# One load for the attention bias of two heads, from a planned order with new durations and new ranks

## The chip, the core and the metric

The kernel runs on one core of a Trainium2 chip. The core has a matmul engine (TensorE, PE in the profile; PEld is its weight load), VectorE (DVE), ScalarE (ACT), GpSimd (POOL) and SyncE (SP), which here issues nearly all transfers to the core's 16 DMA engines. The metric is the time of one execution on the device in microseconds (us); lower is better.

## What is computed

A transformer layer with a conditioned normalization, followed by an adapter, a rotation and a second adapter, for 8 sequences of 512 tokens and 256 features, with 16 heads of 16 features. Cut to what matters:

```
def _L0_cond_ref(src, src_mask, timestep, attention_bias, ...):
    emb = silu(_sin_emb(timestep)) @ W_ada + b_ada
    x = _ln(src) * (1.0 + scale) + shift
    q, k, v = heads of (x @ Wq + bq), (x @ Wk + bk), (x @ Wv + bv)
    scores = jnp.einsum('bhqd,bhkd->bhqk', q / math.sqrt(HEAD_DIM), k)
    scores = scores + attention_bias
    scores = jnp.where(src_mask, -jnp.inf, scores.astype(jnp.float32))
    probs = jax.nn.softmax(scores, axis=-1).astype(v.dtype)
    ctx = jnp.einsum('bhqk,bhkd->bhqd', probs, v)
    x = x + (ctx @ Wo + bo)
    h = _ln(x) * g2 + beta2
    ff = _gelu2(h @ W1 + b1) @ W2 + b2
    return x + ff

x = _L0_cond_ref(x, mask, ...)
x = adapter(x, domain, L1 weights)    # down, gelu, expert of the domain, up, residual, layernorm
x = rotate pairs of features of x by theta and phi
x = adapter(x, domain, L3 weights)
```

`attention_bias` has 8 x 16 x 512 x 512 elements of four bytes, 134 MB; every element is read once. Everything is float32.

## The kernel before

The attention is cut into 128 units: a sequence `b`, a group `g` of four heads and a tile `qt` of 128 queries. A unit's four heads each have a tile of 128 queries x 512 keys. In `attention` (from line 915), a unit goes through these steps, one instruction (or group of them) per head:

- SP loads the head's bias tile into a buffer of the set `BIAS` (line 924, 256 KB a load). `BIAS` (line 298) has 15 buffers of 128 x 512; `dif` are the unit's four.
- POOL adds the mask's large negative numbers, in place (line 928).
- PE makes the scores of the four heads into four PSUM banks (line 936), side by side in strips of 32 rows.
- DVE subtracts scores and bias into the bias buffer and finds the row's extreme, `low` (line 948); ACT takes the exponential there (line 952).
- The probabilities must be turned. For two heads of a unit (none in most of the first sequence) DVE transposes blocks of 32 (line 963, into `tb`) and four DMAs of 128 KB carry them on (line 972, `pT<-tb`). For the others PE transposes (line 987) and ACT or DVE copies the result to `pT` (line 709, the function `evict`). The last of these reads frees the head's bias buffer.
- After every second unit PE multiplies `pT` with the values (line 1013), and DVE and POOL divide by the sums (lines 1026 to 1042).

Between the units lie the projections of the next sequence (`prepare`, from line 785) and, for each half sequence, the rest of the layer (`finish`: lines 1067, 1076, 1083 and 1092 are the feed-forward block, 775 and lines from 1109 the adapters, 717 and 719 the statistics of a normalization, 731 to 739 its application).

The order is written by a planner in the program itself. Each piece of work is a `Task` with a cost for each engine that could do it, a rank, and, for a DMA, the time that its data takes (`data`). `Plan.run` plays the engines through: whenever an engine is free it takes the ready task of the lowest rank whose buffers can be had, and the task's instructions are emitted in the order so found. On the chip every engine then runs its own instructions in exactly that order, and semaphores make it wait for what it needs. So a duration in this list never is a time on the chip: it only decides what is put ahead of what. `AFTER` is how long after a task's end another engine may see its result. `FLIGHT` is how many DMAs may be under way. `Slots.take` gives out the buffer that has been free for longest; a task that needs buffers takes all of them at its start. `Plan.stir`, called at the end, adds to the rank of each task between two bounds a random number of a given seed and width: a list of (seed, low, high, width).

Of the kernel before, what the change touches and what calls it, by code (L numbers as in the profile page):

```python
# [12 lines left out]
F32 = mybir.dt.float32  # L13
# [7 lines left out]
P = 128  # L21
# [59 lines left out]
class Plan:  # L81
# [3 lines left out]
    AFTER = {PE: 0.22, DVE: 0.14, ACT: 0.16, POOL: 0.12, DMA: 3.95}  # L85
# [70 lines left out]
    def run(self, free_at):  # L156
# [14 lines left out]
        while events:  # L171
# [15 lines left out]
            for e in [e for e in free_at if e in idle]:  # L187
# [26 lines left out]
                for b in new:  # L214
                    b.home, b.slot = b.slots.take()
                t.engine, cost = e, t.costs[e]
# [32 lines left out]
def conditioned_sequence_kernel(  # L249
# [22 lines left out]
    nc = tc.nc  # L272
# [25 lines left out]
    BIAS = slots("bias", 15, [P, S])  # L298
# [407 lines left out]
    def evict(pair, r, w, act=0.47, dve=0.6):  # L706

        plan({ACT: act, DVE: dve}, 0, lambda e: (
            nc.scalar.copy(*pair()) if e == ACT else nc.vector.tensor_copy(*pair())), r, w)  # L709

    def statistics(src, src_keys, ts, at=None):
# [3 lines left out]
        for i, (t, key) in enumerate(zip(ts, src_keys)):  # L715
            st = Buffer(ST)
            plan(DVE, 0.33, lambda t=t, st=st: nc.vector.bn_stats(st.t, src.t[:, t, :]),  # L717
                 [key], [st], at=at[i] if at else 0.0)
            plan(DVE, 0.21, lambda t=t, st=st: nc.vector.bn_aggr(mv.t[:, t, :], st.t),
                 [st], [(mv, t)])  # L720
# [64 lines left out]
    def prepare(b):  # L785
# [4 lines left out]
        else:  # L790
            plan(DMA, 0.42, lambda: nc.sync.dma_start(
                res.t, x[b].rearrange("(t p) d -> p t d", p=P)), [], rk, data=1.7)
            plan(DMA, 0.42, lambda: nc.sync.dma_start(
# [120 lines left out]
    def attention(u, n):  # L914
# [6 lines left out]

        dif = [Buffer(BIAS) for _ in range(4)]
        for j in range(4):
            plan(DMA, 0.54, lambda j=j: nc.sync.dma_start(
                dif[j].t, bias[b, 4 * g + j, qt * P : (qt + 1) * P, :]), [], [dif[j]], data=0.84)
# [16 lines left out]
        plan(PE, 0.98, scores, [(qz, par, c) if n else (qz, par, c, "first"), (kT, c)], sc,  # L942
# [8 lines left out]
        for j in range(4):  # L951
            plan(ACT, 0.61, lambda j=j: nc.scalar.activation(  # L952
# [23 lines left out]
        if turned:  # L976
            plan(DMA, 2.75, moved, [(tb, j) for j in range(turned)], [(pT, i)],
# [41 lines left out]
        plan(PE, 1.77, values,  # L1019
# [15 lines left out]
        plan(DVE, 0.21, lambda: nc.vector.reciprocal(of()[:, :, HD], of()[:, :, HD]),  # L1035
# [11 lines left out]
    def feed_forward(res, rk, ts, store=None):  # L1047
# [50 lines left out]
        plan(DVE, 0.1 + 0.3 * n, lambda: nc.vector.tensor_tensor(  # L1098
# [4 lines left out]
    def adapter(b, l, res, rk, ts):  # L1103
# [32 lines left out]
        plan(ACT, 0.27 * n, hidden, [ps, "hid1", "db"], [hid], mode="gelu")  # L1136
# [153 lines left out]
    for n, u in enumerate(units):  # L1290
# [19 lines left out]
        (388521, 59.4, 64.4, 0.5),  # L1310
        (526635, 99.5, 104.5, 0.3),
        (955239, 98.0, 118.0, 0.5),
        (76748, 107.2, 117.2, 0.5),
        (291160, 124.7, 129.7, 1.0),
        (963473, 114.0, 124.0, 0.3),
        (664487, 54.4, 59.4, 0.3),
        (203363, 125.2, 135.2, 0.3),
        (75368, 112.3, 117.3, 0.5),
        (653452, 55.6, 60.6, 0.15),
        (593813, 126.0, 131.0, 1.0),  # L1320
        (573843, 21.5, 41.5, 0.3),
        (961937, 121.3, 131.3, 0.5),
        (875800, 20.4, 25.4, 0.15),
        (637145, 2.0, 12.0, 0.3),
        (952600, 127.6, 137.6, 1.0),
        (260962, 22.0, 27.0, 0.15),
        (38009, 26.2, 36.2, 0.15),
        (272002, 74.3, 84.3, 0.3),
        (911904, 116.2, 156.2, 0.15),
        (541163, 124.1, 129.1, 0.5),  # L1330
        (844975, 78.6, 88.6, 0.3),
        (346962, 121.8, 126.8, 0.5),
        (101166, 97.2, 107.2, 0.15),
        (373769, 121.5, 131.5, 0.3),
        (978427, 78.1, 88.1, 0.5),
        (387854, 121.1, 141.1, 1.0),
        (228221, 124.5, 134.5, 0.5),
        (633691, 29.4, 34.4, 0.3),
        (193779, 129.6, 134.6, 1.0),
        (179418, 94.4, 99.4, 0.15),  # L1340
        (68732, 33.0, 38.0, 1.0),
        (696729, 123.1, 128.1, 0.5),
# [98 lines left out]
```

## Time and profile before

| | us |
|---|---|
| median of 3 runs | 875.85 (873.74 to 878.02) |
| the profiled execution | 876.24 |
| its span, first to last instruction | 874.4 |

The mean clock granted to PE is 0.994 of full speed. The DMA engines move 221.56 MB, at 253 GB/s in the mean. Groups of instructions that the change bears on, with busy time, mean duration of one, idle time of the engine just before them and what ended most of it:

```profile
L928 POOL TENSOR_TENSOR bias<-bias,neg 128x512 f32<-128x512 f32 x512 | 580.3, 1163 | 13.0 <-DMA bias<-in_bias 10.8
L952 ACT ACTIVATE bias<-bias,low 128x512 f32<-128x512 f32 x512 | 344.5, 720 | 37.5 <-DVE low L948 36.6
L948 DVE CUSTOM_DVE_ANT_0 bias<-bank,bias 128x512 f32<-128x512 f32 x512 | 328.7, 680 | 37.3 <-PE bank L936 28.1
...
L963 DVE STREAM_TRANSPOSE tb<-bias 128x512 f32<-128x512 f32 x232 | 155.8, 692 | 3.6 <-ACT bias L952 3.0
L709 ACT COPY pT<-bank 128x512 f32<-128x512 f32 x229 | 126.7, 584 | 29.5 <-PE bank L987 27.2
```

The left part names line, engine and operation, then output and inputs by the program's names (buffer numbers left out) and their shapes. Every engine but PE idles for more than 95 us in all; the waits shown here are idle time of engines that are not the busiest, and cost nothing by themselves.

```profile
PE 77%; ACT 10%; POOL 5%; DVE 4%; DMA 2%; issue 2%; SPq 0%; POOLq 0%; DVEq 0%; ACTq 0%
```

That is the chain of work that ended last, by engine: followed back from the last instruction, at each step to whatever released it or to the instruction before it on its engine.

### The profile page before, as it was taken

The numbers are of one execution on the slowest core, as the hardware profiler recorded it, in microseconds if no ns is written. First come the engines' busy times: TensorE is split into PE (matmuls) and PEld (weight loads), VectorE is DVE, ScalarE is ACT, GpSimd is POOL, SyncE is SP. The second block draws the span as 40 slices with busy tenths as digits, with TensorE's granted clock in tenths as the row PEclk, the third lists the DMA queues.
The fourth block names the chain that finished last, engine by engine and source line by source line (L and its number), as shares of the span: only waits on it lengthen the run. The fifth ranks groups of instructions, "written<-read, shape, count | busy, mean of one in ns | idle before, by whom it ended". The sixth has DMA issues, their size and how long they took to land.

```text
span 874.4 us, 20307 instructions
## 1 busy us (share of the span) xinstructions
PE 855.0 (98%) x6430; PEld 564.5 (65%) x6430; DVE 778.9 (89%) x2132; ACT 744.4 (85%) x1358; POOL 774.9 (89%) x907
## 2 busy tenths in 40 slices
PE   9999999999999999999999999999999999999994
PEld 7656666566766666667666676666666566666783
DVE  3788888989998999999999889999998999999766
ACT  5987879989898998989989897988889798799653
POOL 8699999999899897999889998998999999899432
PEclk9999999999999999999999999999999999999997
DMA  9698886898988899886986978978996979998300
GB/s 294 192 302 280 280 291 208 232 292 263 311 246 269 252 283 298 260 288 227 294 278 226 292 242 252 317 241 282 283 303 191 291 259 283 303 319 259 103 25 24
DMA packets 163936, 221.56 MB, mean 253 GB/s; under 512 B 18819, under 2 KB 93613, under 8 KB 163782
## 3 DMA queue, kind: packets, MB, share of 16 engines
q1 hardware_dynamic: 163786, 220.25, 79.8%
q8 instruction: 51, 0.84, 0.4%
q14 instruction: 55, 0.45, 0.2%
q10 hardware_dynamic: 44, 0.02, 0.0%
HBM read 152.92 MB, written 7.27 MB: 183 GB/s over the span
## 4 chain that ended last, share of the span: by engine, by line
PE 77%; ACT 10%; POOL 5%; DVE 4%; DMA 2%; issue 2%; SPq 0%; POOLq 0%; DVEq 0%; ACTq 0%
PE bank L936 13%; PE bank L1092 12%; PE bank L987 12%; PE bank L1013 10%; PE bank L1067 9%; PE bank L827 6%; PE bank L775 5%; ACT bias L952 3%; POOL bias L928 3%; PE bank L865 2%; PE bank L751 2%; DMA bias<-in_bias 2%; PE bank L1122 2%; PE bank L421 2%; ACT pT L709 1%
## 5 line engine op out<-in xcount | busy, mean ns | idle before, releaser
L928 POOL TENSOR_TENSOR bias<-bias,neg 128x512 f32<-128x512 f32 x512 | 580.3, 1163 | 13.0 <-DMA bias<-in_bias 10.8
L952 ACT ACTIVATE bias<-bias,low 128x512 f32<-128x512 f32 x512 | 344.5, 720 | 37.5 <-DVE low L948 36.6
L948 DVE CUSTOM_DVE_ANT_0 bias<-bank,bias 128x512 f32<-128x512 f32 x512 | 328.7, 680 | 37.3 <-PE bank L936 28.1
L987 PEld LDWEIGHTS bank<-shifted,bias 128*128 128x128 f32 x1120 | 125.4, 141 | 73.6 <-ACT bias L952 28.8
L987 PE MATMUL bank<-shifted,bias 128*128 128x128 f32 x1120 | 157.5, 277 | 5.1 <-ACT pT L709 2.3
L963 DVE STREAM_TRANSPOSE tb<-bias 128x512 f32<-128x512 f32 x232 | 155.8, 692 | 3.6 <-ACT bias L952 3.0
L709 ACT COPY pT<-bank 128x512 f32<-128x512 f32 x229 | 126.7, 584 | 29.5 <-PE bank L987 27.2
L936 PE MATMUL bank<-kT,qz 32*128 32x512 f32 x1024 | 148.7, 640 | 0.0
L1067 PE MATMUL bank<-hT,w 128*128 128x256 f32 (+1 forms) x544 | 127.9, 375 | 0.5 <-ACT hT L761 0.5
L1013 PE MATMUL bank<-pT,v_pad 128*32 128x256 f32 x1120 | 123.0, 382 | 0.0
L1092 PE MATMUL bank<-w,gT 128*128 128x256 f32 x496 | 118.8, 383 | 0.0
L1067 PEld LDWEIGHTS bank<-hT,w 128*128 128x128 f32 x544 | 94.0, 190 | 29.4 <-issue 8.0
L1013 PE MATMUL bank<-pT,v_turn 128*32 128x256 f32 x928 | 111.4, 382 | 0.3 <-issue 0.3
L1092 PEld LDWEIGHTS bank<-w,gT 128*128 128x128 f32 x496 | 89.9, 190 | 22.6 <-issue 9.6
L1013 PEld LDWEIGHTS bank<-pT,v_turn 128*32 128x32 f32 x928 | 49.1, 109 | 50.9 <-issue 7.8
L936 PEld LDWEIGHTS bank<-kT,qz 32*128 32x128 f32 x1024 | 41.9, 182 | 40.6 <-issue 25.9
L1076 ACT ACTIVATE sig<-bank,b1s 128x256 f32<-128x256 f32 (+1 forms) x136 | 55.4, 455 | 6.4 <-PE bank L1067 4.9
L1083 DVE SCALAR_TENSOR_TENSOR gT<-bank,cols,sig 128x256 f32<-128x256 f32 (+1 forms) x128 | 54.2, 462 | 6.5 <-POOL sig L1079 6.0
L1079 POOL TENSOR_SCALAR sig<-sig 128x512 f32<-128x512 f32 (+1 forms) x68 | 40.3, 594 | 20.1 <-ACT sig L1076 13.3
L1013 PEld LDWEIGHTS bank<-pT,v_pad 128*32 128x32 f32 x1120 | 54.6, 109 | 5.3 <-ACT pT L709 1.7
L717 DVE BATCH_NORM_STATS2 st<-res 128x6 f32<-128x256 f32 x128 | 51.5, 409 | 1.5
L725 POOL TENSOR_TENSOR rstd<-rstd,neg_half 128x2 f32<-128x2 f32 (+2 forms) x59 | 43.4, 735 | 4.9
(138 smaller groups left out, 1101.9 us busy)
## 6 DMA issues: line engine op xcount, KB each, us to landing
bias<-in_bias SPq DMA_DIRECT2D x512, 256.0 KB
pT<-tb SPq DMA_DIRECT2D x464, 128.0 KB
out<-res SPq DMA_DIRECT2D x15, 256.0 KB
res<-in_x SPq DMA_DIRECT2D x7, 512.0 KB
value_rows<-v_pad SPq DMA_DIRECT2D x8, 272.0 KB
v_turn<-value_rows SPq DMA_DIRECT2D x8, 272.0 KB
m<-in_mask SPq DMA_DIRECT2D x8, 256.0 KB
mod<-ada_rows SPq DMA_DIRECT2D x8, 256.0 KB
```

The source lines that it names most:

```text
L709: nc.scalar.copy(*pair()) if e == ACT else nc.vector.tensor_copy(*pair())), r, w)
L928: plan(POOL, 1.12, lambda j=j: nc.gpsimd.tensor_tensor(dif[j].t, dif[j].t, negs[qt].t, ALU.add), [negs[qt]], [dif[j]])
L936: nc.tensor.matmul(sc[j].t, qz.t[strip, par, c, qs], kT.t[strip, c, :], start=True, stop=True,)
L948: plan(DVE, 0.61, lambda j=j: nc.vector.tensor_tensor_reduce(dif[j].t, sc[j].t, dif[j].t, -1.0, 3.0e38, ALU.add, ALU.min, low.t[:, j : j + ...
L952: plan(ACT, 0.61, lambda j=j: nc.scalar.activation(dif[j].t, dif[j].t, AF.Exp, bias=low.t[:, j : j + 1], scale=-1.0), [(low, j)], [dif[j]] ...
L963: plan(DVE, 0.62, lambda j=j: nc.vector.transpose(tb.t.rearrange("p (m h k c) -> h p k m c", m=4, h=TURNED, k=NT)[j], dif[j].t.rearrange(" ...
L987: nc.tensor.transpose(ps.t[:, kc, :], dif[j].t[:, kc * P : (kc + 1) * P], ident)
L1013: nc.tensor.matmul(pv.t[32 * j : 32 * j + 32, :], (v_turn if j < turned else v_pad).t[:, at : at + 32], pj, start=(kc == 0), stop=(kc == N ...
L1067: nc.tensor.matmul(ps.t[:, i, :w], w1[:, c, f * P : (f + 1) * P], hT.t[:, c, :w], start=(c == 0), stop=(c == NC - 1),)
L1076: plan(ACT, 0.155 + 0.1 * n, lambda i=i, f=f, ps=ps, sg=sg: nc.scalar.activation(sg.t[:, i, :w], ps.t[:, i, :w], AF.Tanh, bias=b1s[:, f : ...
L1083: plan(DVE, 0.14 + 0.13 * n, lambda i=i, f=f, ps=ps, sg=sg: nc.vector.scalar_tensor_tensor(gT.t[:, f, :w], ps.t[:, i, :w], cols[:, C_B1 + ...
L1092: nc.tensor.matmul(ps.t[:, i, :], gT.t[:, f, i * P : (i + 1) * P], w2[:, f, :], start=(f == 0), stop=(f == NF - 1),)
```

## The change

The 15 bias buffers become slices of one large tile. From the second unit on, one DMA loads the tiles of two heads: the source is two heads of the same 128 queries, and the destination is the large tile with two slices, whose distance is the stride between them, so that any two free slices can be taken. The planner sorts the slots that a task has taken from one set, so that the first is the lower. The first unit still loads head by head. Besides, durations in the planner's list are changed, and the list for `stir` is replaced: 33 entries with windows of 5 to 40 ranks give way to 21, four of which cover all ranks. The engines' instructions are the same in number and shape; their order, and which buffers they use, is what the planner makes of the new list.

```
-    AFTER = {PE: 0.22, DVE: 0.14, ACT: 0.16, POOL: 0.12, DMA: 3.95}
+    AFTER = {PE: 0.26, DVE: 0.14, ACT: 0.16, POOL: 0.12, DMA: 4.35}
...
                 for b in new:
                     b.home, b.slot = b.slots.take()
+                for home in {b.home for b in new}:
+                    mine = [b for b in new if b.home is home]
+                    for b, slot in zip(mine, sorted(b.slot for b in mine)):
+                        b.slot = slot
...
-    BIAS = slots("bias", 15, [P, S])
+    bias_tiles = const.tile([P, 15, S], F32, tag="bias_tiles", name="bias_tiles")
+    BIAS = Slots([bias_tiles[:, i] for i in range(15)])
...
-    def evict(pair, r, w, act=0.47, dve=0.6):
+    def evict(pair, r, w, act=0.485, dve=0.6):
...
-            plan(DVE, 0.21, lambda t=t, st=st: nc.vector.bn_aggr(mv.t[:, t, :], st.t),
+            plan(DVE, 0.11, lambda t=t, st=st: nc.vector.bn_aggr(mv.t[:, t, :], st.t),
...
+        def two_heads(j):
+            low, high = dif[j].slot, dif[j + 1].slot
+            nc.sync.dma_start(
+                bias_tiles[:, low : high + 1 : high - low],
+                bias[b, 4 * g + j : 4 * g + j + 2, qs].rearrange("h q k -> q h k"))
+
         for j in range(4):
-            plan(DMA, 0.54, lambda j=j: nc.sync.dma_start(
-                dif[j].t, bias[b, 4 * g + j, qt * P : (qt + 1) * P, :]), [], [dif[j]], data=0.84)
+            if n == 0:
+                plan(DMA, 0.54, lambda j=j: nc.sync.dma_start(
+                    dif[j].t, bias[b, 4 * g + j, qs, :]), [], [dif[j]], data=0.84)
+            elif j % 2 == 0:
+                plan(DMA, 0.61, lambda j=j: two_heads(j), [], dif[j : j + 2], data=1.68)
...
-        plan(PE, 0.98, scores, [(qz, par, c) if n else (qz, par, c, "first"), (kT, c)], sc,
+        plan(PE, 1.01, scores, [(qz, par, c) if n else (qz, par, c, "first"), (kT, c)], sc,
...
-            plan(ACT, 0.61, lambda j=j: nc.scalar.activation(
+            plan(ACT, 0.62, lambda j=j: nc.scalar.activation(
...
-            plan(DMA, 2.75, moved, [(tb, j) for j in range(turned)], [(pT, i)],
+            plan(DMA, 2.87, moved, [(tb, j) for j in range(turned)], [(pT, i)],
...
-        plan(PE, 1.77, values,
+        plan(PE, 1.83, values,
...
-    plan.stir([
-        (388521, 59.4, 64.4, 0.5),
...
+    plan.stir([
+        (885440, -99.0, 9999.0, 0.3),
+        (794772, -99.0, 9999.0, 0.3),
+        (765284, -99.0, 9999.0, 0.15),
+        (737822, -99.0, 9999.0, 0.15),
+        (607854, 84.8, 124.8, 0.5),
...
```

The other durations that change: the mask load 0.42 to 0.55, the reciprocal (line 1035) 0.21 to 0.11, the feed-forward block's addition (line 1098) 0.1 + 0.3 n to 0.3 n, and the adapter's gelu (line 1130) 0.27 n to 0.32 n, where n is the number of 128-token tiles.

More of the change, by code (lines that the diff above doesn't have):

```diff
@@ L792, in prepare @@
                 res.t, x[b].rearrange("(t p) d -> p t d", p=P)), [], rk, data=1.7)
-            plan(DMA, 0.42, lambda: nc.sync.dma_start(
+            plan(DMA, 0.55, lambda: nc.sync.dma_start(
                 m8.t, mask[b].rearrange("(t p) k -> p t k", p=P)), [], [m8], data=1.1)
@@ L1034, in attention @@
         of = lambda: sb.t.rearrange("p (b e) -> p b e", e=32)
-        plan(DVE, 0.21, lambda: nc.vector.reciprocal(of()[:, :, HD], of()[:, :, HD]),
+        plan(DVE, 0.11, lambda: nc.vector.reciprocal(of()[:, :, HD], of()[:, :, HD]),
              [], [sb])
@@ L1097, in feed_forward @@
                 plan(PE, 0.86, out_sums, [(gT, f0), (gT, f0 + 1), "w2"], [ps], mode="full")
-        plan(DVE, 0.1 + 0.3 * n, lambda: nc.vector.tensor_tensor(
+        plan(DVE, 0.3 * n, lambda: nc.vector.tensor_tensor(
             res.t[:, here], ps.t[:, :n], res.t[:, here], ALU.add), [ps], rk)
@@ L1135, in adapter @@
         plan(PE, 0.52, down, [*xk, "wd"], [ps], mode="down")
-        plan(ACT, 0.27 * n, hidden, [ps, "hid1", "db"], [hid], mode="gelu")
+        plan(ACT, 0.32 * n, hidden, [ps, "hid1", "db"], [hid], mode="gelu")
         def add(ps):
@@ L1309, in conditioned_sequence_kernel @@
     plan.stir([
-        (388521, 59.4, 64.4, 0.5),
[L1311 to L1342, printed above, removed]
+        (885440, -99.0, 9999.0, 0.3),
[3 more added lines that the diff above has]
+        (607854, 84.8, 124.8, 0.5),
+        (886128, 94.3, 99.3, 0.15),
+        (948330, 89.8, 99.8, 0.3),
+        (583505, 119.4, 159.4, 0.3),
+        (217298, 79.9, 89.9, 0.15),
+        (69777, 126.3, 146.3, 1.0),
+        (254646, 84.9, 94.9, 0.15),
+        (197981, 65.4, 85.4, 0.3),
+        (999944, 72.3, 77.3, 0.5),
+        (86346, 123.5, 128.5, 0.15),
+        (242602, 128.7, 133.7, 1.0),
+        (359993, 55.3, 65.3, 0.15),
+        (117736, 99.0, 109.0, 0.5),
+        (110451, 32.2, 37.2, 0.3),
+        (345240, 19.1, 24.1, 0.15),
+        (895446, 69.8, 74.8, 0.15),
+        (983884, 59.5, 69.5, 0.15),
     ])
```

## The prediction

> **What bounds the kernel.** I read the busy times first, then the busy times by stage, then the waits and the issues of the queue that the change touches, and last the chain of work that ended last.
>
> ```profile
> span 874.4 us, 20307 instructions
> PE 855.0 (98%) x6430; PEld 564.5 (65%) x6430; DVE 778.9 (89%) x2132; ACT 744.4 (85%) x1358; POOL 774.9 (89%) x907
> ```
> PE, the matmul engine, is idle for 874.4 - 855.0 = 19.4 us. The Trainium skill ("Perfetto Trace Analysis", Identifying the Most-Contended Engine) warns that matmul busy time is a poor measure and that the weight load's share, 65% here, is a better one; read so, PE would have about 300 us of room. The trace does not bear that out in the middle of the kernel: there the starts of the 256-column matmuls follow each other at an unchanging 215 ns. So I go by the gaps. The busy times by stage (length, then PE, PEld, DVE, ACT, POOL with their counts, clock, DMA share, GB/s) say where PE idles:
>
> ```profile
> 20.00:130.00 110.00, 107.68 (x853) 69.30 (x846) 88.61 (x250) 90.31 (x167) 99.60 (x103) 1.00 0.83 269
> ...
> 610.00:780.00 170.00, 169.66 (x1310) 109.84 (x1309) 160.21 (x430) 151.17 (x269) 159.63 (x175) 1.00 0.87 275
> ...
> 835.00:875.00 40.00, 28.30 (x178) 21.86 (x176) 25.70 (x74) 18.93 (x53) 12.45 (x33) 0.87 0.06 20
> ```
> From 610 to 780 us PE idles 0.34 us. Over 20 to 835 us the stages give 2.32, 1.01, 0.49, 0.99, 0.49, 0.99, 0.34, 0.16 and 0.00: 6.8 us. The last stage has 11.1 us up to the end of the span; 6.6 of them lie after the last matmul ends (867.8), in the closing normalization and store. "Busy" also hides small losses. Taking each matmul's start to the next start, less the pace of its kind (109 ns for 128 columns, 215 for 256, 429 for 512, about 513 for a row-tiled score pair), I count 275 gaps of about 98 ns where the array's tiling changes (27 us), 382 of about 67 ns where it does not (25.6 us, waits that ended just in time), and 37 of over 115 ns (17.7 us, most of the visible idle included). The last two are what a better order can attack: 43 us in all, spread thin.
>
> **The changed transfer.** Its issues and its waits (duration ns: minimum, median, maximum; then waits of the SyncE queue SPq and of POOL, us in total, times, longest):
>
> ```profile
> L924 SPq DMA_DIRECT2D bias<-in_bias x512: 327/382/2149, 4.5 to 811.3; - x171
> ```
> ```profile
> L972 SPq DMA_DIRECT2D pT<-tb x464: 542/599/1527, 65.4 to 821.5; - x155
> ...
>   PEld bank L1013: 0.8, 3
> ```
> ```profile
> L791 SPq DMA_DIRECT2D res<-in_x x7: 374/425/466, 16.8 to 544.9; - x7
> ```
> ```profile
> POOL bias L928 <- DMA bias<-in_bias: 10.8, 12, 2.6
> ```
> ```profile
> SPq L924 <- PE bank L987: 90.2, 53, 6.6
> ```
>
> Part 1, **fewer issues**. 512 loads of one head become 4 (unit 0) and 254 of two heads. From one start to the next on SPq a load of 256 KB takes 436 ns in the median (382 of it the instruction). A 512 KB load of two heads isn't in the trace. The nearest row is L791, 512 KB from HBM in 1 KB rows: 471 ns from start to start. Bounds: 0.43 us, as the mask load L793 (median 384, start to start 430), and 0.87 us, two of today's. I take 0.47, since L791 moves the same bytes to the same 128 partitions. Saved on SPq: 254 x (0.872 - 0.47) = 102 us, between 0 and 112. It lies beside other work almost whole: the queue is not what PE waits for. Behind a waiting bias load stand the pT<-tb transfers of L972, and those made PE's weight loads at L1013 wait only 0.8 us in 3 times. POOL waited 10.8 us for bias loads. The chain of work shows the places where that mattered:
>
> ```profile
> 524.23 4.31 DMA bias<-in_bias
> ...
> 534.00 4.11 DMA bias<-in_bias
> ```
> ```profile
> 603.06 4.77 DMA bias<-in_bias
> ```
> ```profile
> 788.70 2.67 DMA bias<-in_bias
> ```
> PE idled 0.49, 0.99 and 0.16 us in the stages 520 to 545, 545 to 610 and 780 to 800 that hold these: 1.6 us. So SP's relief is worth 0 to 1.6 us; I take -0.8. If PE were not covered by its queue of other matmuls, the whole 15.9 us of these four pieces would be at stake.
>
> Part 2, **the first head waits for the second**. One completion covers both heads, so POOL's add (L928) on the first can't begin before the second has landed. 256 KB at the 317 GB/s of the best slice take 0.83 us, at the mean 253 GB/s 1.04 us. Matching loads and adds by their order, an add starts 3.6 us after its load's issue at the earliest, 4.4 at the 5th percentile, 6.1 at the 25th, 7.5 in the median. With 3.6 us as the latency, some 5% of the heads have less than 0.8 us to spare: 26 x 0.83 = 21 us more waiting for POOL, which has 99.5 us idle. Today 10.8 us of such waiting go with 1.6 us of idle PE, a ratio of 0.15, so PE pays 0 to 3.2 us; I take +1.2, since the new order can ask for the loads earlier. The Trainium skill ("DMA: Bandwidth & Descriptors", Why a DMA increments its semaphore by 16 and not by 1) speaks against the change here: only the full count says that all data have landed, so half a transfer can't be used. That agrees with POOL's wait; by its "Anatomy" figure (about 2 us fixed and 436 GB/s) the second 256 KB would add an estimated 0.6 us and the term would shrink to some +0.9; no run here shows that fixed part alone.
>
> Part 3, **two slots at once**. The 15 slots turn over every 15 x 874.4 / 512 = 25.6 us. SP already waits 90.2 us (53 times) for transposes on PE (L987) to free a slot. A pair needs two: one slot more at 1.71 us a slot. Against a median spare of 7.5 - 3.6 = 3.9 us this is covered for most heads; it costs nothing in my sum and is the second rival. Sorting the slots of a task only renames buffers and banks: nothing, and no instruction is added.
>
> Part 4, **newer durations and redrawn ranks**. No instruction of PE, DVE, ACT or POOL is added or removed; only orders change. The old list was below the trace where I can compare: scores 0.98 against 1.10 us from start to start, values 1.77 against 1.87, exp 0.61 against 0.72 busy; and above it for bn_aggr (0.21 against 0.176 busy). The new entries move the first three towards the rows. Bounds: at best it recovers the 6.8 us in the middle, 4.5 in the last stage (11.1 - 6.6) and a third of the 25.6 us of short gaps, -20 us; at worst it adds as much. I take a tenth of the 43 us, -4.3, because the old order leaves PE nearly nothing from 610 to 780 us and a redraw can't gain there.
>
> **Sum.** -0.8 + 1.2 + 0 - 4.3 = -3.9 us. The profiled execution took 876.24 us: 874.4 of span and 1.8 around it, 0.4 above the median of the runs. Its own sum is 876.24 - 3.9 = 872.3; against the median, 875.85 - 3.9 = 872.0, which I predict.
>
> **Rivals.**
> (R1) The recalibrated order recovers far more: a third of the 43 us, -14 us: 862. For it: 382 short waits mean that the order is often late by little. Against: they are scattered, and most will merely move. Chance 0.13.
> (R2) **The slot ring runs short.** Place: SPq at the bias load, whenever fewer than two slots are free. A quarter of the heads have under 6.1 - 3.6 = 2.5 us to spare, less than 1.71 + 0.83. If these 127 are late by 1.25 us on average, POOL is late by 159 us in total, and at the ratio 0.15 PE by 24 us; half of that, +12 us, if the order makes room: 888. It decides once POOL's waits for bias loads pass its 99.5 us of idle time. For: SP waits for slots already. Against: the four places above cost PE just 1.6 us. Chance 0.20.
> (R3) The redrawn order is worse on the chip than the old one, by the same fifth of the 43 us that a better one could gain, +9 us: 885. For: with 0.34 us idle in 170, the old order is hard to match. Against: durations nearer the trace. Chance 0.12.
> (R4) The change doesn't do what it says: a write with a distance between two slots counts as touching all that lies between, so a load waits for the users of other heads. A third of 15 slots lost on average takes the ring from 25.6 to 17 us, against about 3.6 + 4.4 + 1.4 us (issue to add, add to reduction, reduction to exp, medians but for the first) and the transposes: over 900 us. Against: L972 writes pT in strides between the copies of L709, and waits for its own tb (21.9 us) and hardly for those copies (2.2 us). Chance 0.04.
>
> **How the numbers follow.** My forecast has 0.51, with a range of its own of 866 to 879. A difference of 0.5%, 4.4 us, is about what a measurement of this kernel can tell from none: faster is under 871.5, slower over 880.2. The forecast's centre lies at the edge: 0.24 faster, 0.26 the same, 0.01 slower. R1 adds 0.13 to faster; R2 0.05 to the same and 0.15 to slower; R3 0.04 and 0.08; R4 0.04 to slower. Faster 0.37, same 0.35, slower 0.28. The range that holds 8 in 10 takes most of R1 and the near half of R2 and R3: 863 to 884.
>
> **What would show it.** Right: 258 bias loads of about 0.5 us; POOL's wait for them between 10 and 35 us; PE busy again 850 to 856 us and idle 14 to 20; SP's waits for L987 not far from 90 us. R2: POOL's wait for bias loads above 60 us, DMA's share of the chain above 5%. R3: the waits of PE on ACT and DVE grow with POOL's wait unchanged. R4: bias loads waiting on L948 or L952 of other units throughout. I would be wrong on part 1 if a two-head issue took near 0.9 us, and on part 4 if the short gaps changed by more than a third.

## The result and the profile after

| | before | after |
|---|---|---|
| median, us | 875.70 (873.74 to 878.02, 6 runs) | 880.94 (879.94 to 881.71, 6 runs) |
| span of the profiled execution, us | 874.4 | 879.1 |

The ratio is 1.0049, with a 95% interval of 1.0032 to 1.0066: slower by about half a per cent. The time lies in the range of 863 to 884, but I had forecast 872.0, so the sign was wrong; it is also above 866 to 879, the forecast's own range. Line numbers are higher now: the bias load is L931, POOL's addition L943, the scores L951, the reduction L963, exp L967, the transposition for the DMAs L978, the DMAs L987, the transposes on PE L1002, the copies L714, the division L1041 to L1057.

The page of after, with its span, busy times, chain of waits and DMA issues:

```profile
span 879.1 us, 20145 instructions
...
PE 857.4 (98%) x6430; PEld 563.8 (64%) x6430; DVE 790.0 (90%) x2161; ACT 735.4 (84%) x1329; POOL 776.0 (88%) x907
...
PE 48%; POOL 16%; DVE 13%; DMA 11%; ACT 7%; issue 5%; SPq 1%; POOLq 0%; DVEq 0%; ACTq 0%
...
bias_tiles<-in_bias SPq DMA_DIRECT2D x254, 512.0 KB, 5.9
pT<-tb SPq DMA_DIRECT2D x464, 128.0 KB, 4.5
```

PE idles 879.1 - 857.4 = 21.7 us, 2.3 more than before, and its share of the chain fell from 77 to 48%. DVE has 29 instructions more and ACT 29 fewer. One group of before and the groups of after show which (the columns are those of the groups shown earlier):

```profile
L709 DVE COPY pT<-bank 128x512 f32<-128x512 f32 x51 | 33.9, 674 | 3.2 <-PE bank L987 3.1
```
```profile
L943 POOL TENSOR_TENSOR bias_tiles<-bias_tiles,neg 128x512 f32<-128x512 f32 x512 | 580.3, 1165 | 21.2 <-DMA bias_tiles<-in_bias 16.1
L967 ACT ACTIVATE bias_tiles<-bias_tiles,low 128x512 f32<-128x512 f32 x512 | 345.2, 717 | 50.8 <-DVE low L963 48.4
L963 DVE CUSTOM_DVE_ANT_0 bias_tiles<-bank,bias_tiles 128x512 f32<-128x512 f32 x512 | 329.5, 679 | 37.2 <-POOL bias_tiles L943 16.0
...
L978 DVE STREAM_TRANSPOSE tb<-bias_tiles 128x512 f32<-128x512 f32 x232 | 156.0, 692 | 3.1 <-ACT bias_tiles L967 2.6
...
L714 ACT COPY pT<-bank 128x512 f32<-128x512 f32 x201 | 112.8, 581 | 32.4 <-PE bank L1002 30.5
...
L714 DVE COPY pT<-bank 128x512 f32<-128x512 f32 x79 | 52.7, 676 | 3.3 <-PE bank L1002 3.2
```

None of these groups got slower: the means agree with those of before within 5 ns. The planner gave DVE 28 copies more (79 against 51) and ACT 28 fewer, and ACT now waits 48.4 us for DVE's reduction instead of 36.6. My text held that only orders would change; the planner also chooses the engine of a copy.

The busy times by stage of after (columns as before):

```profile
20.00:130.00 110.00, 107.61 (x804) 68.14 (x797) 90.12 (x251) 86.41 (x159) 98.13 (x104) 0.98 0.80 257
...
610.00:780.00 170.00, 168.53 (x1308) 109.74 (x1301) 161.74 (x438) 147.15 (x262) 157.01 (x172) 1.00 0.88 276
835.00:880.00 45.00, 32.73 (x200) 25.60 (x198) 28.95 (x84) 19.89 (x56) 15.00 (x38) 0.86 0.08 24
```

From 610 to 780 us PE idles 1.47 us where it idled 0.34. Counted as in the prediction, from one matmul's start to the next less its pace: gaps of over 115 ns went from 37 with 17.7 us to 58 with 23.3 us, short gaps within one tiling from 25.5 to 26.1 us, changes of tiling from 27.1 to 25.1 us, and the time after the last matmul stayed at 6.7 us. Together +4.2 us of the span's +4.7. So the loss is some twenty more long gaps spread over the kernel.

Who waits for the changed load, in the waits of after, first of POOL and DVE, then of the SyncE queue (us in total, times, longest):

```profile
POOL bias_tiles L943 <- DMA bias_tiles<-in_bias: 16.1, 15, 3.0
DVE bias_tiles L963 <- POOL bias_tiles L943: 16.0, 22, 3.1
```
```profile
SPq L931 <- PE bank L1002: 99.5, 44, 8.3
SPq L931 <- DVE tb L978: 47.4, 27, 8.1
SPq L987 <- DVE tb L978: 38.5, 29, 3.7
...
SPq L987 <- DMA bias_tiles<-in_bias: 33.1, 44, 2.4
```

The queue's waits of all lines grew from 320 to 420 us, though it has 254 instructions fewer to issue. An addition starts 9.7 us after its load's issue in the median, 2.2 us later than before (7.5): each bias slot is held longer before anything reads it. Yet POOL waits only 5.3 us more for loads. The answer for the line of the load shows its issue and its landing:

```profile
L931 SPq DMA_DIRECT2D bias_tiles<-in_bias x254: 367/436/1957, 9.9 to 807.1; - x127
...
DMA to landing us min/median/max: 3.3/5.9/9.5
```

### The profile page after: what moved, and what is told of

It is laid out like the page before. It is cut to its first block, busy times and chain, and to the rows that moved or that the text cites. A ratio compares the mean times of both kernels' runs of the same rounds, so it can differ in the third digit from the quotient of the medians.

```text
span 879.1 us, 20145 instructions
## 1 busy us (share of the span) xinstructions
PE 857.4 (98%) x6430; PEld 563.8 (64%) x6430; DVE 790.0 (90%) x2161; ACT 735.4 (84%) x1329; POOL 776.0 (88%) x907
## 4 chain that ended last, share of the span: by engine, by line
PE 48%; POOL 16%; DVE 13%; DMA 11%; ACT 7%; issue 5%; SPq 1%; POOLq 0%; DVEq 0%; ACTq 0%
POOL bias_tiles L943 11%; PE bank L1107 8%; PE bank L951 8%; PE bank L1002 8%; PE bank L1082 7%; DMA bias_tiles<-in_bias 7%; PE bank L1028 6%; DVE bias_tiles L963 4%; DMA pT<-tb 3%; ACT bias_tiles L967 3%; PE bank L780 2%; PE bank L832 2%; PE bank L870 2%; DVE st L722 2%; DVE tb L978 2%
## 5 line engine op out<-in xcount | busy, mean ns | idle before, releaser
L943 POOL TENSOR_TENSOR bias_tiles<-bias_tiles,neg 128x512 f32<-128x512 f32 x512 | 580.3, 1165 | 21.2 <-DMA bias_tiles<-in_bias 16.1
L967 ACT ACTIVATE bias_tiles<-bias_tiles,low 128x512 f32<-128x512 f32 x512 | 345.2, 717 | 50.8 <-DVE low L963 48.4
L963 DVE CUSTOM_DVE_ANT_0 bias_tiles<-bank,bias_tiles 128x512 f32<-128x512 f32 x512 | 329.5, 679 | 37.2 <-POOL bias_tiles L943 16.0
L1002 PEld LDWEIGHTS bank<-shifted,bias_tiles 128*128 128x128 f32 x1120 | 127.0, 141 | 72.8 <-issue 21.1
L1002 PE MATMUL bank<-shifted,bias_tiles 128*128 128x128 f32 x1120 | 161.1, 278 | 2.8 <-ACT bias_tiles L967 1.2
L978 DVE STREAM_TRANSPOSE tb<-bias_tiles 128x512 f32<-128x512 f32 x232 | 156.0, 692 | 3.1 <-ACT bias_tiles L967 2.6
L951 PE MATMUL bank<-kT,qz 32*128 32x512 f32 x1024 | 148.6, 643 | 1.1 <-DVE low L963 1.1
L714 ACT COPY pT<-bank 128x512 f32<-128x512 f32 x201 | 112.8, 581 | 32.4 <-PE bank L1002 30.5
L1107 PE MATMUL bank<-w,gT 128*128 128x256 f32 x496 | 120.7, 384 | 0.2 <-DVE gT L1098 0.2
L951 PEld LDWEIGHTS bank<-kT,qz 32*128 32x128 f32 x1024 | 41.5, 183 | 40.0 <-issue 17.1
L714 DVE COPY pT<-bank 128x512 f32<-128x512 f32 x79 | 52.7, 676 | 3.3 <-PE bank L1002 3.2
```

The costliest lines, as they stand in the source:

```text
L943: plan(POOL, 1.12, lambda j=j: nc.gpsimd.tensor_tensor(dif[j].t, dif[j].t, negs[qt].t, ALU.add), [negs[qt]], [dif[j]])
L951: nc.tensor.matmul(sc[j].t, qz.t[strip, par, c, qs], kT.t[strip, c, :], start=True, stop=True,)
L963: plan(DVE, 0.61, lambda j=j: nc.vector.tensor_tensor_reduce(dif[j].t, sc[j].t, dif[j].t, -1.0, 3.0e38, ALU.add, ALU.min, low.t[:, j : j + ...
L967: plan(ACT, 0.62, lambda j=j: nc.scalar.activation(dif[j].t, dif[j].t, AF.Exp, bias=low.t[:, j : j + 1], scale=-1.0), [(low, j)], [dif[j]] ...
L978: plan(DVE, 0.62, lambda j=j: nc.vector.transpose(tb.t.rearrange("p (m h k c) -> h p k m c", m=4, h=TURNED, k=NT)[j], dif[j].t.rearrange(" ...
L1002: nc.tensor.transpose(ps.t[:, kc, :], dif[j].t[:, kc * P : (kc + 1) * P], ident)
```

## The experiments

All ratios are to the kernel before on the same chip, from five rounds. "List" means the durations that the planner is given: old (before), new (after), or mended (new, with two of its entries put back). "Ranks" means the entries given to `stir`. The planner computes an end for each plan; where I quote that, it is the program's own arithmetic and no time of the chip.

### The transfer itself, and the tile

**e1_split**: after's order, with each two-head load issued as two.

```
         def two_heads(j):
             low, high = dif[j].slot, dif[j + 1].slot
-            nc.sync.dma_start(
-                bias_tiles[:, low : high + 1 : high - low],
-                bias[b, 4 * g + j : 4 * g + j + 2, qs].rearrange("h q k -> q h k"))
+            for h, slot in enumerate((low, high)):
+                nc.sync.dma_start(bias_tiles[:, slot], bias[b, 4 * g + j + h, qs, :])
```

> The changed kernel in its own order, slots and ranks, but each load of two heads is issued as two DMAs of 256 KB into the same two slices; nothing else differs. Theory T (the merged transfer costs: the first head waits for the second, and each transfer holds its place in flight longer): the loss of some 4 us goes, 875 to 878 us, and POOL's wait for bias loads falls from 16 to about 10 us. Theory P (the loss is in the planned order: pairs of slots and the ranks redrawn around them): 880 to 884 us, since the order is the same and SP only issues about 100 us more.

Measured: 880.99 us, 1.0053 [1.0034, 1.0072], as slow as after. Its busy times, chain and POOL's wait:

```profile
PE 856.0 (97%) x6430; PEld 562.3 (64%) x6430; DVE 789.6 (90%) x2161; ACT 735.9 (84%) x1329; POOL 775.8 (88%) x907
...
PE 52%; POOL 17%; DVE 13%; ACT 6%; DMA 5%; issue 5%; SPq 1%; POOLq 0%; DVEq 0%; ACTq 0%
```
```profile
POOL bias_tiles L942 <- DMA bias_tiles<-in_bias: 15.1, 12, 4.4
```

Within this order the second head's data cost POOL 16.1 - 15.1 = 1.0 us of waiting before its additions. The edit takes back two things at once, the saved issues and the wait of the first head; together they are worth nothing that the interval can tell. The queue's waits are back at 316 us, and the time does not move: the 100 us that they grew by lie beside other work.

**e2_one_tile**: before, with its buffers as slices of one large tile and the slots of a task sorted.

```
-    BIAS = slots("bias", 15, [P, S])
+    bias_tiles = const.tile([P, 15, S], F32, tag="bias_tiles", name="bias_tiles")
+    BIAS = Slots([bias_tiles[:, i] for i in range(15)])
...
+                for home in {b.home for b in new}:
+                    mine = [b for b in new if b.home is home]
+                    for b, slot in zip(mine, sorted(b.slot for b in mine)):
+                        b.slot = slot
```

> The kernel before with the 15 bias buffers as slices of one large tile and with sorted slots, single loads, old durations, old ranks: the same order on every engine. Both theories: 875 to 877 us, the kernel before. If the large tile itself brings waits between heads (the rival that the change doesn't do what it says): 880 us or more.

Measured: 876.30 us, 0.9998 [0.9985, 1.0011]. The tile and the sorting cost nothing; with e1, what is left is the order.

### One part at a time, without ranks

**e3_single_plain**: after, with loads of one head and no ranks drawn. **e4_pairs_plain**: after with no ranks drawn. **e6_single_plain_13**: e3 with 13 buffers. **e7_single_plain_old**: e3 with the old list. The first diff holds the edit of e3, e6 and e7 (e4 has its last two lines alone), the second that of e6.

```
-            if n == 0:
...
-            elif j % 2 == 0:
-                plan(DMA, 0.61, lambda j=j: two_heads(j), [], dif[j : j + 2], data=1.68)
+            plan(DMA, 0.54, lambda j=j: nc.sync.dma_start(
+                dif[j].t, bias[b, 4 * g + j, qs, :]), [], [dif[j]], data=0.84)
...
-    plan.stir([ ... ])
+    plan.stir([])
```
```
-    bias_tiles = const.tile([P, 15, S], F32, ...)
-    BIAS = Slots([bias_tiles[:, i] for i in range(15)])
+    bias_tiles = const.tile([P, 13, S], F32, ...)
+    BIAS = Slots([bias_tiles[:, i] for i in range(13)])
```

In e7 every changed duration is that of before, `AFTER` too.

> Single loads, new durations, no redrawn ranks at all (an empty list for stir), one large tile. To be set against the next kernel, which has loads of two heads under the same durations and no ranks either. Theory P: ranks are worth much, so it is slower than the kernel before by 5 to 20 us: 881 to 896. Theory T says the same of this kernel.

> Loads of two heads, new durations, no redrawn ranks. Theory P: a pair of slots has to be free at once, so without ranks made for it the plan is worse by 8 to 20 us than with single loads under the same durations. Theory T: worse by about the 4 to 5 us that separate the changed kernel from the one before. If pairs cost nothing: the same as the single loads within 2 us.

> As e3 (single loads, new durations, no ranks, 897.3 us there), but with 13 bias buffers in place of 15. Theory P in its narrower form (a pair needs two slots at once and holds both until the later head is done, as if the ring had about two slots less): about what pairs cost, 904 to 914 us against 908.5 of e4. If the number of slots is not what pairs cost: 895 to 900 us.

> Single loads, old durations, no ranks. Against e3 this shows what the new durations alone do, and against the kernel before what its ranks were worth. If durations nearer to the trace make a better order: slower than e3's 897.3 by 3 us or more. If one order without ranks is as good as another: within 5 us of e3 on either side. In both cases 10 to 25 us slower than the kernel before.

| | load, list | us | ratio |
|---|---|---|---|
| e7 | one head, old | 884.95 | 1.0126 [1.0104, 1.0147] |
| e3 | one head, new | 897.31 | 1.0242 [1.0216, 1.0268] |
| e6 | one head, new, 13 buffers | 900.41 | 1.0287 [1.0269, 1.0305] |
| e4 | two heads, new | 908.47 | 1.0360 [1.0338, 1.0382] |

Three things follow. Ranks matter more than anything else here: after's are worth 908.5 - 880.9 = 27.5 us to it, before's some 10 us. Unranked pairs are 11.2 us slower than unranked single loads; the waits of e4's SyncE queue show where it stands:

```profile
SPq L931 <- PE bank L1002: 105.5, 50, 7.5
SPq L931 <- DVE tb L978: 90.9, 51, 5.4
```

It stands at the load, waiting for slots, 196 us in all in these two rows, where after has 147. But two buffers fewer cost single loads only 3 to 4 us (e6; 3.1 between the medians, 0.45% between the ratios), less than I expected; a smaller ring alone isn't as dear as pairs. And the new list made the unranked order worse than the old list did (e3 against e7), the first sign against part 4. Each of these is one order, though, and a different order can be some us off by luck.

### Pairs in the old order

**e5_old_order_merged** and **e9_old_order_merged**: before's list, ranks and order; where two loads of a unit follow each other in the queue and nobody reads the first in between, one load of two heads stands at the place of the second. That gives 98 of the 254 pairs. In e5 the slots were exchanged so that the bias of some heads was overwritten before it was read, so its time isn't read; e9 deals the slots anew in the order of the plan's times.

```
+    for n, four in loads.items():
+        for (t0, dif, two_heads, j), (t1, _, _, k) in (four[:2], four[2:]):
+            ...
+            takes.append((t1.start, 1, [dif[j], dif[k]]))
+            t0.emit = lambda e: None
+            t1.emit = lambda e, two_heads=two_heads, j=j: two_heads(j)
...
+    for _, taken, buffers in sorted(events, key=lambda e: e[:2]):
+        if taken:
+            slots_of = sorted(free.pop(0) for _ in buffers)
+            for buffer, slot in zip(buffers, slots_of):
+                buffer.slot = slot
+        else:
+            free.append(buffers[0].slot)
```

> The kernel before in its own order, ranks, durations and single slots, where 98 of the 254 pairs of loads that follow each other directly on SP are issued as one DMA of two heads at the place of the second (where the two slots stand the wrong way round, they are swapped). Theory P (the loss lies in the order that pairs of slots force, not in the transfer): 875 to 878 us, the kernel before. Theory T (a transfer of two heads costs by itself): some 2 us more, 878 or above. If relief of SP were worth anything: below 874.

> The kernel before in its own order, ranks and durations; 98 of the 254 pairs of loads, those that follow each other directly on SP, are issued as one DMA of two heads at the place of the second, the slots being dealt out again so that every pair takes two that are free. Transfer costs by itself: some 2 us more than before. Both theory P and theory D: 875 to 878 us. If relief of SP were worth anything: below 874.

Measured: e5 914.14 us, 1.0445 [1.041, 1.048], not read; e9 882.62 us, 1.0067 [1.0044, 1.0090]. The waits of e9's SyncE queue, where L931 is the load of two heads and L936 that of one:

```profile
SPq L931 <- PE bank L999: 58.3, 18, 8.6
SPq L936 <- PE bank L999: 45.5, 32, 4.6
```

The 98 merged loads wait 58.3 us for slots in 18 waits of 3.2 us each, the 316 single ones 45.5 us in 32 waits of 1.4 us. This kernel is 5.9 us slower than before, with no new list and no new rank. That is more than each of my forecasts: 875 to 878 us where the order or the list is to blame, some 2 us more where the transfer is. In an order that was made for single loads, pairs cost more than in one made for them. The edit also holds the first head back, so this is no clean price of the pair.

### The list: what it says of two small instructions

**e8_single_new_tuned**: new list, loads of one head, and ranks searched for this form: random entries, each kept where the planner's own end came earlier with it. The load is that of e3, and the 21 entries become 45.

```
     plan.stir([
-        (885440, -99.0, 9999.0, 0.3),
+        (770124, -99.0, 9999.0, 0.15),
...
```

> Single loads, the new durations, and ranks of my own drawn until the plan under these durations ends at 861.1, as the changed kernel's plan does (861.0); 45 entries for stir. Theory D (the loss comes from two of the new durations: bn_aggr and the reciprocal at 0.11 in place of 0.21, where the trace shows 0.53 and 0.60 us for a statistics or transposition with the dependent instruction behind it, the new list having 0.44 and 0.48): the plan is blind to 19 us of DVE, so the kernel is as slow as the changed one, 878 to 882 us, though it loads head by head. Theory P (pairs of slots are what costs): as fast as the kernel before or faster, 868 to 876.

Measured: 880.59 us, 1.0042 [1.0018, 1.0065]. Single loads with the new list are as slow as after. A part of this loss may be the clock of PE: seven of the eight runs had a mean granted clock of 0.985 to 0.991, the eighth had 0.996 and took 877.19 us, and before had 0.994 in the median on this chip. In e16 below, of the same kind, the clock is that of before. The pairs therefore aren't needed for most of the loss; the list is suspect. I looked at the two durations that were nearly halved, statistics' `bn_aggr` and the reciprocal, both 0.21 to 0.11. The timeline of DVE in after, two places (start us, duration us, then engine, line, operation and tiles):

```profile
240.39 0.43 DVE L722 BATCH_NORM_STATS2 st<-res 128x6 f32<-128x256 f32 x1
240.86 0.18 DVE L724 BATCH_NORM_AGGREGATE mv<-st 128x2 f32<-128x6 f32 x1
240.96 0.40 DVE L722 BATCH_NORM_STATS2 st<-res 128x6 f32<-128x256 f32 x1
241.39 0.18 DVE L724 BATCH_NORM_AGGREGATE mv<-st 128x2 f32<-128x6 f32 x1
241.50 0.69 DVE L963 CUSTOM_DVE_ANT_0 bias_tiles<-bank,bias_tiles 128x512 f32<-128x512 f32 x1
```
```profile
247.12 0.44 DVE L1041 STREAM_TRANSPOSE pvs<-bank 128x256 f32<-128x256 f32 x1
247.59 0.21 DVE L1050 RECIPROCAL pvs<-pvs 128x8 f32<-128x8 f32 x1
247.80 0.71 DVE L978 STREAM_TRANSPOSE tb<-bias_tiles 128x512 f32<-128x512 f32 x1
```

In these rows an instruction that needs the one just before it starts only after that has ended: 0.47 and 0.43 us after its start. One that doesn't need it starts before the other ends: 0.10 us after `bn_aggr`, whose own record is 0.18 us long. Over the trace of before, the medians from start to start are 343 ns from one `bn_stats` to another, 430 from `bn_stats` to the `bn_aggr` that needs it, 99 from `bn_aggr` to the next. So the pair takes 430 + 99 = 0.53 us. The old list counts 0.33 + 0.21 = 0.54, the new one 0.33 + 0.11 = 0.44. The transposition and its reciprocal take 478 + 121 = 0.60 us; the old list counts 0.37 + 0.21 = 0.58, the new one 0.48. The new 0.11 is the pace of the small instruction alone; the wait before it has no place in the list any more. With 128 and 64 of them, DVE is planned short by about 0.09 x 128 + 0.12 x 64 = 19 us, on an engine that is 90% busy. The Trainium skill ("VectorE: DVE Perf Modes", The DRAIN you can't avoid) says that after an operation the pipe empties before the next one starts, and that one that is not held starts earlier. The 430 against 343 ns would fit that, but the section does not tie it to needing the result, and it gives no figure for such a pair.

**e10_single_mended** and **e11_pairs_mended**: these two durations back at 0.21, the others new, and ranks searched for each form in the same way (40 and 45 entries). The first entry is shown for e10; e11 begins with (972950, -99.0, 9999.0, 0.3). The loads are those of e3 and of after.

```
-            plan(DVE, 0.11, lambda t=t, st=st: nc.vector.bn_aggr(mv.t[:, t, :], st.t),
+            plan(DVE, 0.21, lambda t=t, st=st: nc.vector.bn_aggr(mv.t[:, t, :], st.t),
...
-        plan(DVE, 0.11, lambda: nc.vector.reciprocal(of()[:, :, HD], of()[:, :, HD]),
+        plan(DVE, 0.21, lambda: nc.vector.reciprocal(of()[:, :, HD], of()[:, :, HD]),
     plan.stir([
-        (885440, -99.0, 9999.0, 0.3),
+        (631987, -99.0, 9999.0, 0.15),
...
```

> As e8 (single loads, ranks of my own, the same length of search), but bn_aggr and the reciprocal stand in the list at 0.21 again; all other new durations stay. The plan ends at 865.5. With this list the order of the kernel before ends at 867.5 and that of the changed kernel at 872.1, 4.6 apart where the chip's spans are 4.7 apart. Theory D: 0.2% faster than the kernel before, a ratio of 0.994 to 1.001, and at least 0.3% faster than e8. If these two durations are not the cause: as slow as e8, a ratio of 1.003 or more.

> As e10, but with loads of two heads, as in the changed kernel; ranks of my own from a search of the same length. The plan ends at 866.1. Theory D: the changed kernel's loss goes although its transfers stay, a ratio of 0.995 to 1.002. Theory P (loads of two heads cost whatever the list): 1.004 or more.

**e12_single_long**, **e13_pairs_long**: e10 and e11 with the search carried on (58 and 62 entries). **e14_single_b**, **e15_pairs_b**: the same list of durations, searched from other seeds (37 and 44 entries; e15 begins with (508491, -99.0, 9999.0, 0.3)). The edit of e12 against e10, and of e14 against e10:

```
     plan.stir([
...
         (513839, 133.7, 143.7, 1),
+        (728315, 22.5, 27.5, 0.15),
+        (513702, 7.5, 12.5, 0.15),
...
```
```
     plan.stir([
-        (631987, -99.0, 9999.0, 0.15),
+        (575445, -99.0, 9999.0, 0.15),
...
```

> Single loads with the mended list (bn_aggr and reciprocal at 0.21), the search carried on from another draw; the plan ends at 863.0, 2.5 below e10's. Theory D: a ratio of 0.995 to 1.000, below e10's 1.0003.

> Loads of two heads with the mended list, the search carried on from e11's ranks; the plan ends at 863.9, 2.2 below e11's. If loads of two heads cost the chip something that the plan doesn't hold: 0.2 to 0.4% slower than e12. If e11's 0.3% over e10 was the draw: within 0.15% of e12.

> Single loads, mended list, ranks from another start of the search; the plan ends at 866.3, 0.8 above e10's. Expected a ratio of 0.998 to 1.003, as e10.

> Loads of two heads, mended list, ranks from another start of the search; the plan ends at 867.5, 1.3 above e11's. If loads of two heads cost the chip something beyond the plan: a ratio of 1.003 to 1.006, and 0.2 to 0.4% over e14 after the plans' difference of 0.14%. If e11 was the draw: within 0.15% of e14 after that difference.

**e16_single_new_b**, **e17_single_new_c**, **e18_pairs_new_b**: the new list again, from other seeds (30, 32 and 42 entries; e17 begins with 694618, e18 with 506954). The edit of e16 against e8:

```
     plan.stir([
-        (770124, -99.0, 9999.0, 0.15),
+        (865480, -99.0, 9999.0, 0.15),
...
```

> A second order of e8's kind: single loads, the new durations as they stand, ranks of my own; the plan ends at 861.4, and strictly replayed with the two durations mended at 870.6. Theory D: a ratio of 1.003 to 1.007. If e8 was only an unlucky draw: as the three mended orders with single loads, 0.999 to 1.003 (their mean is 1.0015).

> A third order of e8's kind; the plan ends at 862.7, replayed with the two durations mended at 872.4. Theory D: a ratio of 1.004 to 1.009. If the two durations don't matter: 0.999 to 1.003.

> A second order of the changed kernel's kind: loads of two heads, the new durations as they stand, ranks of my own; the plan ends at 863.6, replayed with the two durations mended at 873.7. Theory D with a small cost of the transfers: a ratio of 1.006 to 1.011, above the three mended orders of two heads (mean 1.0041). If the two durations don't matter: 1.002 to 1.005.

The last columns are the DVE instructions and the total that PE and its weight load waited for DVE, summed over all rows of the waits:

| load, list | run | us | ratio | plan's own end | DVE instr. | PE waits for DVE, us |
|---|---|---|---|---|---|---|
| one head, old | before | 875.70 | 1 | 853.5 | 2132 | 43.2 |
| one head, new | e8 | 880.59 | 1.0042 [1.0018, 1.0065] | 861.1 | 2163 | 61.4 |
| one head, new | e16 | 882.34 | 1.0057 [1.0042, 1.0071] | 861.4 | 2157 | 56.4 |
| one head, new | e17 | 881.83 | 1.0052 [1.0039, 1.0066] | 862.7 | 2149 | 51.2 |
| one head, mended | e10 | 876.72 | 1.0003 [0.9990, 1.0016] | 865.5 | 2147 | 49.1 |
| one head, mended | e12 | 874.67 | 0.9988 [0.9980, 0.9997] | 863.0 | 2156 | 49.4 |
| one head, mended | e14 | 880.18 | 1.0053 [1.0040, 1.0066] | 866.3 | 2150 | 44.2 |
| two heads, new | after | 880.94 | 1.0049 [1.0032, 1.0066] | 861.0 | 2161 | 56.7 |
| two heads, new | e18 | 883.53 | 1.0078 [1.0063, 1.0094] | 863.6 | 2161 | 54.5 |
| two heads, mended | e11 | 878.82 | 1.0032 [1.0020, 1.0045] | 866.1 | 2141 | 61.9 |
| two heads, mended | e13 | 877.30 | 1.0022 [1.0006, 1.0039] | 863.9 | 2146 | 56.5 |
| two heads, mended | e15 | 882.16 | 1.0069 [1.0056, 1.0082] | 867.5 | 2143 | 54.9 |

The means by group are 1.0050 (one head, new), 1.0015 (one head, mended), 1.0064 (two heads, new) and 1.0041 (two heads, mended). So in these means the two durations are worth 0.35% with single loads and 0.2% with pairs. The search was not equally long on both sides: without e12 and e13, which were searched on, it is 0.22 and 0.13%. Pairs cost 0.13% with the new list and 0.26% with the mended one, where each of the three pairs of searches has the same sign (0.29, 0.34, 0.16). That is 1.2 to 2.3 us for pairs and 2 to 3 us for the list. Orders of one group differ by up to 0.65% (e12 and e14), so three of a group don't settle such a size. Three results missed what I had expected: e14 and e15 came out slower, and e11 lies between its two forecasts. The signs agree in both comparisons, no more.

The plan's own end says more. I also put each order's instructions through the planner's rules under one list: by the new list after's order ends 5.2 us ahead of before's, by the mended one 4.6 us behind it, and on the chip its span is 4.7 us longer. Before's order ends at 866.2 under the new list and at 867.5 under the mended one. Set against that, the five orders searched under the new list promise to be 2.6 to 5.2 us faster than before, and by their ratios are 3.7 to 6.8 us slower: the plan errs by 8.1 to 9.8 us. The six searched under the mended list promise 0 to 4.5 us and end between 1.1 us faster and 6.0 us slower: it errs by 2.3 to 6.0 us. The two lists differ in nothing but the two durations, and the two ranges do not meet, so these entries misled the planner by some 4 to 5 us. That is arithmetic with durations, chosen after the result was known. The error that is left under the mended list is of the kind to be expected of any order that was picked because a list flatters it. No run searched ranks anew under the old list, so how much a new search alone loses against before is not known.

The best of them is e12, by its page:

```profile
span 872.8 us, 20273 instructions
...
PE 854.7 (98%) x6430; PEld 562.5 (64%) x6430; DVE 786.7 (90%) x2156; ACT 736.2 (84%) x1334; POOL 774.2 (89%) x907
...
PE 63%; POOL 16%; ACT 10%; DVE 5%; issue 4%; DMA 3%; SPq 0%; POOLq 0%; DVEq 0%; ACTq 0%
```

DVE's share of the chain is 5% and that of DMA 3%, against 13 and 11% in after. At 0.9988 [0.9980, 0.9997] it is just ahead of before, by 1.0 us, with loads of one head. It is the best of three draws of its group, and a gain this small could be the luck of the draw.

## Why the prediction was wrong in its sign

**Part 1, fewer issues (-0.8): the mechanism held, and no gain can be seen.** The 254 issues took 436 ns each in the median, near the 425 of L791, from which I had taken 471 from start to start. e1 puts the 254 issues back and changes the ratio by 0.0004, a tenth of its interval. It also lets the first head go, so it tests the sum of parts 1 and 2, +0.4 in my reckoning, and can't tell them apart. The queue had time to spare, as the text said.

**Part 2, the first head waits for the second (+1.2): right in kind, too large.** I reckoned 21 us more waiting for POOL. It is 5.3 us more than before, and only 1.0 us of it goes when e1 lets the first head land alone. A part of the excess was a misread row: in the trace of before the earliest addition starts 3.1 us after its load's issue, not 3.6, and by the same reckoning 11 heads and not 26 would have been late, 9 us in all. POOL's 16.1 us lie in the 10 to 35 that were named. The figure that I set beside this term (the Trainium skill, "DMA: Bandwidth & Descriptors", Anatomy of one DMA) is given there for transfers that GpSimd issues; SP issues these, and no run tells whether it holds for them.

**Part 3, two slots at once (0): mis-sized.** A median spare of 3.9 us should have covered a slot taken 1.71 us early. The slot is held 2.2 us longer and the chain's DMA share rose from 2 to 11%, above the mark of 5% set for R2, but POOL's wait is far under R2's 60 us. The groups with the same list put pairs at 1.2 to 2.3 us, little against the spread within a group and far from R2's 12; 98 pairs forced into the old order cost 5.9 us (e9). In after, what pairs cost sits in the order that they force on the planner, since splitting the transfers in that order (e1) returns none of it, though it takes the chain's DMA share back to 5%. A share of the chain was a poor mark for a price: e16 and e17, with single loads, have 9%.

**Part 4, newer durations and redrawn ranks (-4.3): the step that failed.** It took "newer" for "nearer the trace". For the scores, values and exp the rows supported that. For `bn_aggr` I compared the list's 0.21 with a busy time of 0.176 and called the old entry too high. What a list of durations must hold is the time from one start to the next, with the wait for the instruction before: 0.53 us for the pair, which the old list had right at 0.54. The rows that would have shown it, `bn_stats` and `bn_aggr` side by side, were in the timeline of before, where the `bn_aggr` starts 0.46 us after the `bn_stats`:

```profile
413.08 0.43 DVE L717 BATCH_NORM_STATS2 st<-res 128x6 f32<-128x256 f32 x1
...
413.54 0.18 DVE L719 BATCH_NORM_AGGREGATE mv<-st 128x2 f32<-128x6 f32 x1
413.64 0.84 DVE L1083 SCALAR_TENSOR_TENSOR gT<-bank,cols,sig 128x256 f32<-128x256 f32 x2
```

The reciprocal was cut as well and I didn't look at it. e8, e16 and e17 hold this term by itself, the new list and newly drawn ranks without a single pair (the ranks are mine, not after's): they are slower than before by 0.42 to 0.57%, which is +3.7 to +5.0 us where the sum had -4.3. That the two durations are a reason is supported by the rows of the timeline, by the plan's errors under the two lists and by e10 and e12, against e14. The two last columns of the table fit by halves: DVE has more instructions under the new list with pairs (2161 against 2141 to 2146), but with single loads the groups overlap; PE waits longer for DVE with single loads (51.2 to 61.4 us against 44.2 to 49.4), but with pairs the groups overlap. Whether the other changed durations add to the loss, or ranks searched for longer would do away with it, stays open. The size is open as well.

Taken at face value, the means add up from before upwards so: +1.3 us for single loads in a newly searched order with the mended list, +3.1 for the two durations, +1.2 for pairs, together 5.6 us, the mean of the two orders with pairs and the new list; after itself is the better of these at +4.3 (0.49% of 875.7). That the time still fell into 863 to 884 is owed to the room that was left for the rivals, not to the forecast's sum.

**The rivals.** R3, a redrawn order that is worse on the chip, is what happened, at half its 9 us; I had given it 0.12. Its marks were met in part: PE's waits for DVE rose from 43.2 to 56.7 us, while those for ACT fell from 91.9 to 81.9. R2 has a small part. R1 is out, and e2 excludes R4. PE's busy time and idle time (857.4 and 21.7 us) left the 850 to 856 and 14 to 20 that would have shown the forecast right. The short gaps did not change by a third, as the mark for part 4 had it; the loss lies in the long ones, which I hadn't named as a mark.

## What to carry to other kernels

An entry of a scheduler's list is checked against starts, not busy times: from the instruction before to this one, and from this one to the next, separately for a successor that needs the result. In a kernel whose order is planned and tuned, a change of form is compared with several newly searched orders on both sides, since single orders here differ by 0.65%, more than the change itself. And an issue saved on a queue that waits anyway was worth nothing that these runs can tell, while a transfer that takes two buffers at once asks for them earlier and holds them longer.

## What the runs showed of the hardware

- A load of 512 KB for two heads takes SP 436 ns to issue in after, only 54 ns more than one of 256 KB in before (382 ns). It lands after 5.9 us in the median there, against 3.8 us in e3 and 4.4 us in e8 for 256 KB; but the order decides much of that, since in e9, which has both kinds, the difference is small:

```profile
bias_tiles<-in_bias SPq DMA_DIRECT2D x316, 256.0 KB, 4.4
bias_tiles<-in_bias SPq DMA_DIRECT2D x98, 512.0 KB, 4.7
```

- The clock of PE can fall to half in the middle of a busy kernel. The busy times of after in two stretches of the answer, the clock in the third column from the right:

```profile
75.50:79.00 3.50, 3.50 (x17) 1.73 (x16) 2.93 (x8) 0.73 (x2) 3.50 (x4) 0.51 0.83 285
```
```profile
72.00:75.50 3.50, 2.42 (x27) 1.75 (x24) 3.50 (x10) 3.35 (x6) 3.50 (x4) 1.00 0.81 260
```

  From 75.5 to 79 us the granted clock was 0.51, and a group of scores took 2.09 us instead of 1.14. In the 3.5 us before, PE was busy for 2.42 us. The Trainium skill ("TensorE: Matmul & The Clock Gate", What's actually happening) puts the half clock after at least one idle window of about 3.4 us; here the length fits and the condition does not, since PE was busy for most of it. Nor does the same idle time always do it: from 70 to 75.5 us PE is busy for 4.10 us in after and for 4.05 us in e1, which keeps its full clock. It isn't the cause of the loss: e1 has the same order, no such stretch, and a span of 878.9 us.
- A change of the array's tiling costs PE about 98 ns (27 us over 275 changes in before).
